# A graph layer on one core: rows of numbers for the comparisons moved to PSUM, 26 groups gathered in place of 20

## The chip, the cores and the metric

The kernel runs on one core of a Trainium2 chip. The metric is the time of one execution in microseconds of the device (us). Three runs of the kernel before took 490.9, 492.47 and 494.97 us; the median is 492.47. The core's engines are TensorE (PE in the profile, with PEld for its weight loads), VectorE (DVE), ScalarE (ACT), GpSimd (POOL) and SyncE (SP, which here only issues DMAs). Each runs its own instructions in order and waits for others by semaphores.

## The reference

One layer of a graph network over 6250 nodes with 64 features and 206250 edges, which are sorted by their destination.

```python
h = jnp.maximum(_layernorm(x, axis=-1), 0.0)
msg = h[src] + edge_feat                       # 206250 x 64
agg = jax.ops.segment_sum(msg, dst, num_segments=6250)
x = x + jax.nn.relu(agg @ W1 + b1) @ W2 + b2
```

So every node sums, over the edges that end in it, the edge's own features and the row of h of the edge's source.

## The kernel before

The edges lie in G = 202 groups of 1024. The sum over the rows of h is made in two ways. For the first GA = 182 groups it is made by **counting**: a matrix that says how often node s is the source of an edge that ends in node d is built on the chip and multiplied by h. For the last GP = 20 groups the rows of h are **gathered** by indirect DMAs that add them onto the edges' features in SBUF.

*Counting.* The nodes are taken in windows of V = 3, each with up to 128 edges in a tile. For a tile VectorE makes two one-hot matrices by comparing the edges' keys with rows of numbers 0, 1, 2, ... (`iota_lo`, 128 wide, and `iota_key`, 148 wide): `hot_lo` marks the low seven bits of the source, `hot_key` the window's node and the high bits (line 858). One pair of comparisons makes three steps of ST = 6 tiles, a batch; both hot tiles have two buffers. TensorE multiplies the two, which gives the tile's counts (`pc`, line 868), ScalarE copies the counts of a step into a ring (line 871). A step is one `count(b, s)`. A block is BT = 84 tiles, so 14 steps, and covers 252 nodes; there are NW = 23 blocks, the last with BL = 56 tiles (10 steps), 318 steps in all. In the block after, TensorE multiplies h by the counts (`multiply`, line 888, 49 products a block, into `pv`, which has two buffers in PSUM), spread over the first seven steps; VectorE adds `pv` to the sums in SBUF at step 10 (`add_products`, line 900).

*Edge features.* For the counted groups they are loaded in chunks of 42 nodes (`load`, 384 KB each, four buffers), summed by TensorE with one-hot matrices (`chunk_hot` line 427, `chunk_sum` line 439, into `bank`) and placed into `pv` (`chunk_place`, line 461).

*Gathered groups.* A group's edge rows are loaded (`load_h`, 256 KB, tile `pfeat`, four buffers, so two pairs of groups), then GpSimd issues eight gathers that add rows of h from the table in HBM (`fetch_h`, line 301 through `gather`). A pair of groups is then summed by TensorE (`features_h`, `sum_groups`, line 489), placed (`place_groups`, line 508) and added (`add_sums`). Right behind a pair's sum the loads and gathers of the pair after the next are put in the queues.

*Other gathers.* GpSimd also fetches, through the same queue and line, the words that hold the keys (`fetch_pair`, two gathers for 256 windows, `words`; `unpack_pair` and `turn_pair` make keys of them) and the nodes of the chunks' edges (`fetch_dst`, `dstq`).

*The order* is written out by hand. A loop over the steps issues `count`, then the products, placings and additions that stand at fixed steps of a block (`SUMS`, `PLACES`, `PRODUCTS`, `ADDED`; names with `_L`, and `LAST`, `LATE`, are for the last block). For GpSimd the kernel keeps a clock of its own: each gather has an assumed cost (`GATHER_US`, `WORDS_US`), each step `STEP_US`, and a pair's sum is put at the first step of a few allowed ones (`GROUPS`) at which its gathers would have landed. The clock only sets the order of instructions in the program; on the chip the engines wait for semaphores. Since TensorE runs in order, a sum that waits for its gathers holds all behind it. At the end come the rest of the products, the last sums and the two dense products of the last blocks of nodes (`mlp_hidden` line 936, `mlp_rows` line 943).

[...]

Of the kernel before, what the change touches and what calls it, by code (L numbers as in the profile page):

```python
# [9 lines left out]
F32 = mybir.dt.float32  # L10
BF16 = mybir.dt.bfloat16
# [3 lines left out]
AF = mybir.ActivationFunctionType  # L15
# [4 lines left out]
P = 128  # L20
N = 6250
E = 206250
# [12 lines left out]
J = 8  # L35
# [17 lines left out]

GP = 20
PQ = 4
PK = J // PQ
GA = G - GP
# [14 lines left out]
BT = 84  # L74
BN = V * BT
NH = BN // 2
NW = 23
BL = 56
NWIN = (NW - 1) * BT + BL - NX
NS = NWIN * V  # L80
IC = -(-NWIN // P)
# [26 lines left out]

HEAD_US = 1.5
STEP_US = 1.25  # L110
GATHER_US = 2.3
WORDS_US = 2.9
LAND_US = 4.0
NEED_P = N - 31 * GP - 6
OPEN = 30
# [6 lines left out]
def gnn_kernel(ctx: ExitStack, tc: tile.TileContext, x, src_t, dst_t, dst_g, edge, w1, b1, w2, b2, out):  # L122
# [177 lines left out]
    def gather(rows, source, index, op=OP.bypass):  # L300
        nc.gpsimd.indirect_dma_start(out=rows, out_offset=None, in_=source,  # L301
                                     in_offset=bass.IndirectOffsetOnAxis(ap=index, axis=0), compute_op=op)
# [96 lines left out]

    bank = ps.tile([P, GB * D], F32, name="bank", bufs=1)  # L400
    nc.vector.memset(bank, 0.0)
    units = []
    for b in range(NW):
        c0, c1 = (start[b] // CN, min(start[b + 1], NS) // CN)
# [240 lines left out]
    def by_quarters(t0, t1):  # L645
        rows = src_s.bitcast(F32)
        for t in range(t0, t1):
            own = slice(t * QP, (t + 1) * QP)
            px = ps.tile([P, 512], F32, tag="pv", name="psrcq")[:, :GP * PK]
            for b in range(PQ):  # L650
                nc.tensor.matmul(px, spread[own, b].rearrange("p a c -> p (a c)"), rows[own, :, b, :],
                                 start=(b == 0), stop=(b == PQ - 1))
            nc.scalar.activation(src_p[:, :, t], px.rearrange("p (g k) -> p g k", k=PK), AF.Copy)
# [28 lines left out]
    bad = small.tile([P, CHECKED + 2 * NT + 4], F32, name="bad")  # L682
    nc.vector.memset(bad, 0.0)
    sums_bad = bad[:, CHECKED + 2 * NT:]
    junk = late.tile([P, RC * CT], BF16, name="junk")

    def checked(of, p, low, high, at):
        shape = of.shape[1:]
# [156 lines left out]
    def count(b, s):  # L845

        t = b * BT + s * ST
        n = b * STEPS + s
        r = n - opens(n)
        if r == 0:  # L850
            n = min(ST * (1 if n == 0 else R - 1 if n < R else R), TILES - t)
            assert all(at_col.get(c % KR) == c for c in range(t, t + n)), t
            opened[0] = t + n
            hots[:] = [work.tile([P, R * ST, P], BF16, name="hot_lo"),
                       work.tile([P, R * ST, K + 1], BF16, name="hot_key")]
            for k, (hot, iota_k) in enumerate(zip(hots, (iota_lo, iota_key))):
                m = hot.shape[2] // 2
                nc.vector.tensor_tensor(  # L858
                    hot[:, :n].rearrange("p t (m o) -> p t m o", o=2),
                    iota_k.rearrange("p (m o) -> p m o", o=2).unsqueeze(1).to_broadcast([P, n, m, 2]),  # L860
                    keys[:, k, t % KR:t % KR + n, :].unsqueeze(2).to_broadcast([P, n, m, 2]), op=OP.is_equal)
                if k and 0 < b * STEPS + s < OPEN:
                    nc.vector.memset(spare, 0.0)
        hot_lo, hot_key = (hot[:, r * ST:(r + 1) * ST, :] for hot in hots)
        pc = ps.tile([P, 2, 512], F32, tag="pc", name="pc")
        for j in range(ST):
            k, m = divmod(j, ST // 2)
            nc.tensor.matmul(pc[:, k, m * K:(m + 1) * K], hot_lo[:, j, :], hot_key[:, j, :K],  # L868
                             start=True, stop=True)
        half, i = divmod(s, (STEPS if b < NW - 1 else STEPS_L) // 2)  # L870
        nc.scalar.activation(  # L871
            ring[:, (2 * b + half) % 3, :, i * ST * V:(i + 1) * ST * V].rearrange("p h (k m) -> p h k m", k=2),
            pc[:, :, :ST // 2 * K].rearrange("p k (m h) -> p h k m", h=HI), AF.Copy)

    def open_pv(b):
        pvs[b] = [ps.tile([P, 512], F32, tag="pv", name="pv")[:, :BN], 0]

    def multiply(b, upto):

# [99 lines left out]
    def fetch_h(g):  # L979
        if g >= G:  # L980
            return
        if g not in parts_of:
            load_h(g)
        for j in range(J):
            queue.append((GATHER_US, lambda j=j: gather(
                parts_of[g][:, j, :], table[:, :], src_p[:, g - GA, j // PK, j % PK:j % PK + 1], OP.add)))
        queue.append((0.0, lambda: fetched.setdefault(g, pool[0])))
# [102 lines left out]
    def clock(n):  # L1090

        return n * HEAD_US if n < STEPS else STEPS * HEAD_US + (n - STEPS) * STEP_US
# [6 lines left out]

    SUMS, PLACES, LAYERS = (7, 10, 13), 3, (8, 11)  # L1100
    PRODUCTS = (5, 12, 19, 26, 33, 41, HI)
    PRODUCTS_L = (8, 18, 28, 39, HI)
    ADDED, LOADED = 10, 2
    LAST, LATE, SUMS_L = (3, 8), 7, (6, 8)
    ADDS = (6, 7)
    GROUPS, PLACED = (0, 1, 2, 4), (1, 2, 4, 5)
    ready = []
# [34 lines left out]
    for n, (b, s) in enumerate(steps):  # L1142
        for f in before.get(n, []):
            f()
        count(b, s)
        upto = PRODUCTS if b < NW - 1 else PRODUCTS_L
        if b >= 1 and s < len(upto):
            multiply(b - 1, upto[s])
        if b >= 1 and s == (PLACES if b < NW - 1 else 2):
            for u in places[b - 1]:  # L1150
                chunk_place(u)
        if b >= 1 and s == (ADDED if b < NW - 1 else LATE):
            add_products(b - 1)
            if b - 1 > SB:
                ready.append(b - 1)
        k = n - (first_step[SB + 1] + ADDED + 1)
        if 0 <= k < 3 * -(-NX // 4) and k % 3 == 0:
            add_seconds(k // 3 * 4)
            if k // 3 == -(-NX // 4) - 1:
                ready[:0] = range(SB + 1)  # L1160
        if s == LOADED or b == NW - 2 and s == STEPS // 2:
            for m in ready[:len(LAYERS)] if b < NW - 1 else ready + [NW - 2, NW - 1]:
                if m not in xs:
                    residual(m)
        if b == NW - 1 and s == STEPS // 2:
            for m in range(NW, NB):
                if m not in queued:
                    residual(m)
        if s in (LAYERS if b < NW - 1 else LAST) and ready and ready[0] in xs:
            mlp(ready.pop(0), n)  # L1170
        for f in later.pop(n, []):
            f()
        if n >= 3:
            if h_next < G and s in GROUPS and fetched.get(h_next + 1, 1e9) + LAND_US <= clock(n):
                features_h(h_next)
                n_placed = next((k for k in range(n + 2, last) if b == NW - 1 or steps[k][1] in PLACED), last)
                at(n_placed, place_groups, h_next)
                h_next += GB
                add_later(next((k for k in range(n_placed + 3, last) if steps[k][1] in ADDS or steps[k][0] == NW - 1 and
                                steps[k][1] != LATE), last))  # L1180
            if n == 3:
                pool[0] = clock(n - 1) + OPENING_US
            pool_until(clock(n) + LAND_US)
# [155 lines left out]
```

## Time and profile before

| what | value |
|---|---|
| median of three runs | 492.47 us |
| the profiled execution's own time | 489.07 us |
| its span in the profile | 487.2 us |
| mean granted clock of TensorE | 0.954 |
| gathers of h (line 301, `pfeat`) | 160 |
| counts copied by ScalarE (line 871) | 318 |
| batches of comparisons (line 858) | 107 of each kind |

The profile is that of one execution. A row of a group gives the line of the code, the engine, the operation, the tile written and the tiles read, the shape and how often; behind the first bar the busy time in us and the mean in ns; behind the second the idle time of the engine just before, and what ended it. A row of the timeline gives start and duration in us, and in brackets the idle time before it. The slices cut the span into 40 equal parts of 12.2 us, one digit each, in tenths busy.

### The profile page before, as it was taken

What the parts mean: (1) busy time and instruction counts of PE and PEld (TensorE: products, weight loads), DVE (VectorE), ACT (ScalarE), POOL (GpSimd) and SP (SyncE); (2) the same over time, 40 slices, a digit from 0 to 9 for tenths busy, and PEclk for the clock granted to TensorE, in tenths of its full rate; (3) what the DMA queues carried; (4) which work ended last, traced back from release to release, by engine and by line L of the source; (5) the groups of instructions that cost most, each with busy time, mean ns of one, the idle gap of its engine ahead of it and who ended that gap; (6) DMA issues with size and microseconds to landing.
All of it is one profiled execution on the core that took longest, in us unless ns stands there. A gap on an engine that the chain in (4) does not pass through costs nothing.

```text
span 487.2 us, 17218 instructions
## 1 busy us (share of the span) xinstructions
PE 424.2 (87%) x7301; PEld 374.8 (77%) x7302; DVE 415.1 (85%) x561; ACT 366.0 (75%) x607; POOL 388.3 (80%) x239
## 2 busy tenths in 40 slices
PE   3156798998988999999999999989999999999894
PEld 3055687886886888888988978878888888888783
DVE  7888989879999798988998889888998899998751
ACT  3727889878877788788898789777887787786650
POOL 7787888888888888888888888888888888888000
PEclk9655699999999999999999999999999999999998
DMA  9959367378366585784784784675775775764700
GB/s 237 238 172 300 74 147 193 76 180 192 69 167 155 145 228 122 176 230 105 192 220 98 172 228 94 170 201 125 187 187 124 201 179 122 203 158 93 213 13 16
DMA packets 122378, 77.98 MB, mean 160 GB/s; under 512 B 34768, under 2 KB 120728, under 8 KB 122072
## 3 DMA queue, kind: packets, MB, share of 16 engines
q1 hardware_dynamic: 97464, 66.88, 47.1%
q0 software_dynamic: 24592, 9.19, 15.0%
q8 instruction: 59, 0.97, 0.8%
q10 hardware_dynamic: 240, 0.75, 0.5%
q14 instruction: 23, 0.19, 0.1%
HBM read 72.80 MB, written 3.99 MB: 158 GB/s over the span
## 4 chain that ended last, share of the span: by engine, by line
PE 68%; ACT 13%; DMA 6%; issue 5%; DVE 4%; POOL 3%; DVEq 0%; ACTq 0%; POOLq 0%
PE pv L888 26%; PE pc L868 22%; PE bank L439 11%; ACT counts L871 9%; POOL rows L301 3%; DMA feat<-in_edge 3%; PE po L943 2%; PE pv L461 2%; DMA dstq<-in_dst_g,cols_i 2%; ACT junk L694 1%; PE ph L936 1%; PE bank L489 1%; DVE hot_key L858 1%; DVE hot_lo L858 1%; DMA firsts_i<-in_dst_g 1%
## 5 line engine op out<-in xcount | busy, mean ns | idle before, releaser
L301 POOL DMA_INDIRECT pfeat<-table,src_p x160 | 334.0, 2088 | 49.7 <-issue 43.0
L871 ACT ACTIVATE counts<-pc 128x882 fp32r<-128x882 f32 x318 | 282.1, 916 | 49.1 <-PE pc L868 39.8
L868 PE MATMUL pc<-hot_key,hot_lo 128*128 128x147 bf16 x1908 | 179.2, 232 | 22.9 <-ACT counts L871 13.6
L858 DVE TENSOR_TENSOR hot_lo<-iota_lo,keys 128x2304 bf16<-128x2304 bf16 (+1 forms) x107 | 143.8, 1344 | 36.2 <-PE pc L868 29.0
L888 PE MATMUL pv<-counts,h 128*128 128x252 f32 (+1 forms) x1127 | 171.0, 292 | 0.2
L868 PEld LDWEIGHTS <-hot_lo 128*128 128x128 bf16 x1908 | 130.5, 100 | 45.4 <-issue 24.2
L858 DVE TENSOR_TENSOR hot_key<-iota_key,keys 128x2664 bf16<-128x2664 bf16 (+1 forms) x107 | 163.3, 1526 | 0.0
L888 PEld LDWEIGHTS pv<-counts,h 128*128 128x128 f32 x1127 | 143.5, 190 | 0.6 <-ACT counts L871 0.5
L439 PE MATMUL bank<-feat,hot 128*21 128x64 f32 x3240 | 69.0, 222 | 5.9 <-issue 3.0
L439 PEld LDWEIGHTS bank<-feat,hot 128*21 128x21 f32 x3240 | 52.3, 101 | 18.3 <-issue 6.8
L427 DVE TENSOR_TENSOR hot<-rel,iota 128x504 f32<-128x504 bf16 x68 | 45.6, 671 | 0.1
L442 ACT ACTIVATE by_node<-bank 128x128 f32<-128x128 f32 x68 | 19.0, 280 | 18.4 <-PE bank L439 12.4
L301 POOL DMA_INDIRECT words<-packed,first_i x15 | 20.8, 1385 | 4.6 <-issue 3.4
L301 POOL DMA_INDIRECT rows<-in_dst_g,row_i x15 | 17.4, 1162 | 5.2 <-issue 4.0
L943 PE MATMUL po<-w2s,hid 128*126 128x64 f32 (+2 forms) x100 | 16.8, 288 | 1.7 <-ACT hid L938 1.2
L943 PEld LDWEIGHTS po<-w2s,hid 128*126 128x126 f32 (+2 forms) x100 | 13.5, 192 | 5.7 <-ACT hid L938 1.9
L936 PE MATMUL ph<-sums,w1s 128*128 128x252 f32 (+2 forms) x50 | 16.1, 404 | 0.2 <-ACT y L949 0.2
L900 DVE TENSOR_TENSOR sums<-sums,pv 128x252 f32<-128x252 f32 (+4 forms) x31 | 9.8, 339 | 6.7 <-PE pv L888 5.9
L492 ACT ACTIVATE by_group<-bank 128x128 f32<-128x128 f32 x10 | 2.8, 277 | 15.1 <-PE bank L489 11.1
L938 ACT ACTIVATE hid<-ph,b1s 128x252 f32<-128x252 f32 (+2 forms) x25 | 11.6, 464 | 2.3 <-PE ph L936 2.3
L461 PE MATMUL pv<-select,by_node 128*64 128x42 f32 (+1 forms) x272 | 12.6, 234 | 0.0
L461 PEld LDWEIGHTS pv<-select,by_node 128*64 128x64 f32 x272 | 9.9, 137 | 3.0
(202 smaller groups left out, 252.3 us busy)
## 6 DMA issues: line engine op xcount, KB each, us to landing
feat<-in_edge SPq DMA_DIRECT2D x135, 384.0 KB
pfeat<-in_edge SPq DMA_DIRECT2D x20, 256.0 KB
pfeat<-table,src_p POOLq DMA_INDIRECT x160
xl<-in_x SPq DMA_DIRECT2D x2, 768.0 KB
xs<-in_x SPq DMA_DIRECT2D x23, 63.0 KB
out_y<-y SPq DMA_DIRECT2D x23, 63.0 KB
dstn<-in_dst_g SPq DMA_DIRECT2D x1, 1024.0 KB
table<-xl SPq DMA_DIRECT2D x1, 800.0 KB
```

The source lines that it names most:

```text
L301: nc.gpsimd.indirect_dma_start(out=rows, out_offset=None, in_=source, in_offset=bass.IndirectOffsetOnAxis(ap=index, axis=0), compute_op=op)
L427: nc.vector.tensor_tensor(hot_of[u][:, :n].rearrange("p c j w -> p (c j) w"), rel[:, c:c + n].rearrange("p c q k -> p (c q k)").unsqueeze( ...
L439: nc.tensor.matmul(bank[q * QP:q * QP + WQ, i * D:(i + 1) * D], hot[:, i, j, :], feat[i][:, j, :], start=(k == 0), stop=(k == JP - 1))
L442: nc.scalar.activation(by_node[u][:, :n].rearrange("p c d -> p (c d)"), bank[:, :n * D], AF.Copy)
L461: nc.tensor.matmul(pvs[b][0][i * D:(i + 1) * D, k:k + z - a], of[:, i, :], select[:, a - low:z - low], start=False, stop=False)
L858: nc.vector.tensor_tensor(hot[:, :n].rearrange("p t (m o) -> p t m o", o=2), iota_k.rearrange("p (m o) -> p m o", o=2).unsqueeze(1).to_bro ...
L868: nc.tensor.matmul(pc[:, k, m * K:(m + 1) * K], hot_lo[:, j, :], hot_key[:, j, :K], start=True, stop=True)
L871: nc.scalar.activation(ring[:, (2 * b + half) % 3, :, i * ST * V:(i + 1) * ST * V].rearrange("p h (k m) -> p h k m", k=2), pc[:, :, :ST // ...
L888: nc.tensor.matmul(pv[:, :2 * half].rearrange("p (k n) -> p k n", k=2), h2[:, h, :], of[:, :, h, :half], start=(h == 0), stop=(h == HI - 1))
L936: nc.tensor.matmul(ph[:, :n], w1s, agg[:, start[b]:start[b + 1]], start=True, stop=True)
L938: nc.scalar.activation(outs[b][:, :n], ph[:, :n], AF.Relu, bias=b1s)
L943: nc.tensor.matmul(po[:pairs[b], k, :], outs[b][:, k:2 * pairs[b]:2], w2s, start=True, stop=True)
```

## The change

Three things are changed together.

First, the numbers of `iota_lo` and `iota_key` are also written to PSUM, as 2-byte numbers: in the head TensorE turns the rows into columns by a product with ones, ScalarE copies the columns to SBUF, and TensorE transposes them into a tile `iotas` of one bank. The two comparisons of a count read their first input from there; the keys, their second input, and the outputs stay in SBUF. The bank comes from `pv`, which has one buffer from now on.

Second, GP is 26. The groups that are counted are 176 in place of 182, the blocks NW = 22, and the last has BL = 84 tiles like all others: 308 steps. The last block's own schedule becomes that of the other blocks, with `LATE` at step 11. In the last block a pair's sum may stand at any step above `LOADED`. The assumed costs of the clock go from 2.3 to 1.6 us for a gather and from 2.9 to 1.2 for a pair of words.

Third, in the last group, whose edges end within it, the gathers whose 128 rows are all padding are left out: 4 of its 8.

```diff
-GP = 20
+GP = 26
...
-NW = 23
-BL = 56
+NW = 22
+BL = 84
...
-GATHER_US = 2.3
-WORDS_US = 2.9
+GATHER_US = 1.6
+WORDS_US = 1.2
...
     bank = ps.tile([P, GB * D], F32, name="bank", bufs=1)
     nc.vector.memset(bank, 0.0)
+    iotas = ps.tile([P, P + K + 1], BF16, name="iotas", bufs=1)
+    col = ps.tile([P, 3, P], F32, tag="pc", name="pcol")
+    cols_of = late.tile([P, 3, P], BF16, name="iota_cols")
+    m = K + 1 - P
+    for k, of in enumerate((iota_lo, iota_key[:, :P], iota_key[:, P:])):
+        n = of.shape[1]
+        nc.tensor.matmul(col[:n, k, :], of[0:1, :], onesb[0:1, :], start=True, stop=True)
+        nc.scalar.activation(cols_of[:n, k, :], col[:n, k, :], AF.Copy)
+        nc.tensor.transpose(iotas[:, k * P:k * P + n], cols_of[:n, k, :], identb[:n, :n])
...
-            px = ps.tile([P, 512], F32, tag="pv", name="psrcq")[:, :GP * PK]
+            px = ps.tile([P, 512], F32, tag="pv", name="psrcq", bufs=1)[:, :GP * PK]
...
-            for k, (hot, iota_k) in enumerate(zip(hots, (iota_lo, iota_key))):
+            for k, (hot, iota_k) in enumerate(zip(hots, (iotas[:, :P], iotas[:, P:]))):
...
-        pvs[b] = [ps.tile([P, 512], F32, tag="pv", name="pv")[:, :BN], 0]
+        pvs[b] = [ps.tile([P, 512], F32, tag="pv", name="pv", bufs=1)[:, :BN], 0]
...
         for j in range(J):
+            if g * P * J + j // PK * P * PK + j % PK >= E:
+                continue
             queue.append((GATHER_US, lambda j=j: gather(
...
-    PRODUCTS_L = (8, 18, 28, 39, HI)
+    PRODUCTS_L = PRODUCTS
     ADDED, LOADED = 10, 2
-    LAST, LATE, SUMS_L = (3, 8), 7, (6, 8)
+    LAST, LATE, SUMS_L = (5, 12), 11, SUMS
...
-        if b >= 1 and s == (PLACES if b < NW - 1 else 2):
+        if b >= 1 and s == PLACES:
...
-            if h_next < G and s in GROUPS and fetched.get(h_next + 1, 1e9) + LAND_US <= clock(n):
+            if h_next < G and (s in GROUPS or b == NW - 1 and s > LOADED) and fetched.get(h_next + 1, 1e9) + LAND_US <= clock(n):
```

(One more line makes a scratch tile of ScalarE's large enough for 26 groups.)

More of the change, by code (lines that the diff above doesn't have):

```diff
@@ L684, in gnn_kernel @@
     sums_bad = bad[:, CHECKED + 2 * NT:]
-    junk = late.tile([P, RC * CT], BF16, name="junk")
+    junk = late.tile([P, max(RC * CT, 2 * GP * J)], BF16, name="junk")
     def checked(of, p, low, high, at):
```

## The prediction

> **What bounds the kernel now.** I read the page's busy times and slices first, then the chain, then the costliest groups, then the windows and the timeline around single gathers.
>
> ```profile
> span 487.2 us, 17218 instructions
> PE 424.2 (87%) x7301; PEld 374.8 (77%) x7302; DVE 415.1 (85%) x561; ACT 366.0 (75%) x607; POOL 388.3 (80%) x239
> ...
> PE   3156798998988999999999999989999999999894
> ...
> POOL 7787888888888888888888888888888888888000
> ...
> PE 68%; ACT 13%; DMA 6%; issue 5%; DVE 4%; POOL 3%; DVEq 0%; ACTq 0%; POOLq 0%
> ```
>
> From the fifth slice on TensorE is 90% busy, and the chain that ended last runs through it for two thirds: TensorE sets the end. GpSimd is 80% busy, but its last digit stands three slices before the end: it has some 36 us of room, and no more.
>
> ```profile
> 407.00:456.00 49.00, 44.95 (x851) 39.71 (x840) 43.20 (x57) 37.59 (x59) 38.96 (x19) 1.00 0.64 157
> ```
>
> These columns are PE, PEld, DVE, ACT, POOL busy, then the granted clock. In a late stretch TensorE idles 4.05 of 49 us, at full clock; what a stall costs there can hardly be won back.
>
> ```profile
> L301 POOL DMA_INDIRECT pfeat<-table,src_p x160 | 334.0, 2088 | 49.7 <-issue 43.0 <-PE pc L868 2.1 <-DMA pfeat<-table,src_p 1.8
> L858 DVE TENSOR_TENSOR hot_key<-iota_key,keys 128x2664 bf16<-128x2664 bf16 x105 | 161.6, 1539 | 0.0
> L858 DVE TENSOR_TENSOR hot_lo<-iota_lo,keys 128x2304 bf16<-128x2304 bf16 x105 | 142.3, 1355 | 36.0 <-PE pc L868 29.0 <-issue 3.6 <-ACT counts L871 1.8
> ```
>
> 160 gathers of h take 2.09 us each and 0.30 between two. The timeline shows why 2.09:
>
> ```profile
> 17.43 1.82 DVE L545 TENSOR_REDUCE stat<-xl 128x25 f32<-128x1600 f32 x1 [1.19 <-DMA xl<-in_x]
> 18.51 0.95 POOL L301 DMA_INDIRECT rows<-in_dst_g,row_i  x1 [0.30 <-ACT inrow L317]
> ...
> 20.13 1.82 DVE L550 TENSOR_TENSOR xl<-xl,stat 128x1600 f32<-128x1600 f32 x1
> 21.07 1.70 POOL L301 DMA_INDIRECT rows<-in_dst_g,row_i  x1 [0.30 <-issue]
> ...
> 107.17 1.55 POOL L301 DMA_INDIRECT pfeat<-table,src_p  x1 [0.30 <-issue]
> ...
> 213.87 1.54 DVE L858 TENSOR_TENSOR hot_key<-iota_key,keys 128x2664 bf16<-128x2664 bf16 x1
> 214.17 2.66 POOL L301 DMA_INDIRECT pfeat<-table,src_p  x1 [0.30 <-issue]
> ...
> 446.74 0.68 DVE L427 TENSOR_TENSOR hot<-rel,iota 128x504 f32<-128x504 bf16 x1
> 447.10 1.74 POOL L301 DMA_INDIRECT pfeat<-table,src_p  x1 [0.30 <-issue]
> ```
>
> A gather that begins inside a reduction, which reads one tensor, takes its usual 0.95. One that begins inside a subtraction of two SBUF tensors takes 1.70: it ends 0.82 after that operation. An adding gather with no VectorE work at all takes 1.55. Inside hot_key (ends 215.41) it ends at 216.83, 1.42 later; inside hot (ends 447.42) at 448.84, 1.42 later again. So an adding gather costs 1.54, and one that meets a VectorE operation with two SBUF inputs waits out that operation. Over 160 gathers the waiting is 334.0 - 160 x 1.54 = 87.6 us.
>
> **The change part by part.** *Rows in PSUM.* The two comparisons of a count get their first input from PSUM and keep one SBUF input, like the reduction above. I take it that they no longer hold a gather, and that they keep their 1355 and 1539 ns. No row shows 2-byte numbers read from PSUM; the nearest are 4-byte ones:
>
> ```profile
> L900 DVE TENSOR_TENSOR sums<-sums,pv 128x126 f32<-128x126 f32 x14 | 3.4, 282 | 1.9 <-PE pv L888 1.1 <-issue 0.8
> L928 DVE TENSOR_TENSOR xs<-xs,b2s 126x128 f32<-126x128 f32 x23 | 6.5, 282 | 0.0
> L427 DVE TENSOR_TENSOR hot<-rel,iota 128x504 f32<-128x504 bf16 x67 | 45.2, 675 | 0.1
> L479 DVE TENSOR_TENSOR hotp<-rel_p,iota 128x336 f32<-128x336 f32 x10 | 5.0, 501 | 0.4 <-issue 0.4
> ```
>
> 126 numbers with one input from PSUM and 128 from SBUF alone both take 282 ns: the place costs nothing there. Lower bound: no change. Upper bound: one number at a time, (675 - 501) / 168 = 1.036 ns each, against hot_lo's 1355 / 2304 = 0.59. I take the lower (the rows with PSUM are nearest); the upper is a rival.
>
> [...]
>
> Making the rows adds three products, three copies and three transposes to the head, where TensorE is 10 to 60% busy (first slices 3, 1, 5, 6) and the chain runs through GpSimd's row gathers: cost 0, at most 2 us if the copies push ScalarE's first work. For the bank that the rows take, pv has one buffer. Its next block opens at step 0, four steps after the sums were taken out at step 10; four steps are over 5 us, the two additions under 1. Cost 0; if VectorE runs late, under 1 us a block. The turning of src_p in the head shares that one buffer: four short copies in a row, under 1 us.
>
> *Ten steps less.* Blocks have 14 steps; the last had 10 and is gone.
>
> ```profile
> 406.73 0.65 PE L489 MATMUL bank<-pfeat,hotp 128*21 128x64 f32 x32
> ...
> 456.04 0.92 ACT L871 ACTIVATE counts<-pc 128x882 fp32r<-128x882 f32 x1
> ...
> 470.23 0.91 ACT L871 ACTIVATE counts<-pc 128x882 fp32r<-128x882 f32 x1
> ...
> L508 PE MATMUL placed<-sel,by_group 128*64 128x52 f32 x40 | 3.2, 240 | 0.0
> L888 PE MATMUL pv<-counts,h 128*128 128x252 f32 x1078 | 165.0, 293 | 0.1
> L888 PE MATMUL pv<-counts,h 128*128 128x180 f32 x49 | 6.0, 278 | 0.1
> ```
>
> The first count of that block is at 456.04 and its tenth at 470.23: 14.19 / 9 = 1.58 a step, 15.8 in all. Six more groups are three more pairs, each a sum of 0.65 and a placing of 3.2 / 10 = 0.32. Before the last block 8 of 10 pairs had been summed; now it is 13 of 13: five more, 5 x 0.97 = 4.9. In the tail 49 products of full width replace narrow ones: 49 x (165.0 / 1078 - 6.0 / 49) = +1.5; a pair's sum and placing leave it, -1.0. The last block's products, placings, sums and layers now stand at the steps of every other block: their cost is inside the mean step, 0 here. Edge rows only move from chunks (135 to 131 of 384 KB) to groups (20 to 26 of 256 KB), the same bytes. Against the profiled execution's 489.07, with nobody waiting: 489.07 - 15.8 + 4.9 + 0.5 = **478.7**.
>
> *The gathers.* They were 160 and are 26 x 8 - 4 = 204, the four of the padding left out (4 x 1.84 = 7.4 us at the very end of the queue). Now GpSimd's queue matters. In the order of the instructions the sums of pairs stand after 47, 85, 113, 142, 173, 211, 239, 271, 309 and 318 counts; in the changed kernel after 43, 58, 85, 100, 127, 143, 169, 187, 211, 229, 253, 271 and 295. TensorE takes its work in order: if a pair has not landed, everything behind its sum waits, products, counts, and with them ScalarE and VectorE.
>
> ```profile
> 24.32 0.95 POOL L301 DMA_INDIRECT words<-packed,first_i  x1 [0.30 <-issue]
> ...
> 45.43 1.59 POOL L301 DMA_INDIRECT pfeat<-table,src_p  x1 [1.30 <-ACT counts L871]
> 47.32 6.05 POOL L301 DMA_INDIRECT pfeat<-table,src_p  x1 [0.30 <-issue]
> ...
> 449.14 2.30 POOL L301 DMA_INDIRECT pfeat<-table,src_p  x1 [0.30 <-issue]
> ...
> 26.74 0.51 ACT L317 ACTIVATE inrow<-rows,nhalf 128x256 bf16<-128x256 int32 x1 [1.72 <-DMA rows<-in_dst_g,row_i]
> ```
>
> The twelfth pair, at count 271, decides. Its last gather is the 192nd. From 45.43: 192 x (1.54 + 0.30) = 353.3; 13 other gathers of words and nodes stand ahead of it in the queue, 13 x 1.25 = 16.3. What still has two SBUF inputs still holds some: hot is 45.2 us of the 406 in which gathers run, so 11% of them, 21, meet one and wait about half of it, 0.34: 7 us; smaller operations (xs, y, hotp, sel) 2 more. Together 9; ends are 0 and twice that. Sum 45.4 + 353.3 + 16.3 + 9 = 424.0. Landing: the row gather that ended at 22.77 let its reader start at 26.74, 4.0 later, with four times the bytes; I take 2.5, between 0 and 4. Landed at **426.5**.
>
> ```profile
> 106.77 0.64 PE L489 MATMUL bank<-pfeat,hotp 128*21 128x64 f32 x32
> ...
> 107.69 1.34 SPq L972 DMA_DIRECT2D pfeat<-in_edge  x2
> ```
>
> Each pair adds into tiles that the pair two before has freed; SyncE asks for the new rows 0.3 us after that sum. The first sum stands at count 43, some 5 us ahead of 106.77, and GpSimd is through two pairs at 45.4 + 32 x 1.84 + 1.25, near 106: cost 0, at most 3.
>
> TensorE reached count 271 at 406.73, with seven pairs behind it; with eleven it is there at 406.73 + 4 x 0.97 = 410.6. It waits 15.9. (Most of this falls at count 229, where ten pairs are due, the rest at 271.) The thirteenth pair has 12 gathers, some 23 us; TensorE needs it 24 steps later, over 30 us: no further wait. The words for the keys come behind the same gathers and get late by no more than the sums.
>
> After a wait ScalarE and VectorE have their two buffers ready, so a little comes back: 3 of the 4.05 us that TensorE idles in the late stretch. 478.7 + 15.9 - 3 = 491.6, on the scale of the profiled execution. That one lies 0.7% under the median of the runs shown (492.47; lowest 490.9), so 3.4 go on top: **495**.
>
> **The rivals.** *The gathers keep up* (faster). No hold at all, quick landing: 45.4 + 353.3 + 16.3 = 415.0 against 410.6, a wait of 4.4 that the slack takes back: 478.7 to 483, with the 3.4 up to 487; I put 483. For it: the gather at 107.17, and hot_lo and hot_key are 303.9 of VectorE's 415.1 us. Against it: the gather inside hot at 447.10, which the change leaves as it is. It needs a hold under 1 us in all.
>
> *One element at a time* (slower). Comparisons from PSUM take 675 + 1800 x 1.036 = 2540 and 675 + 2160 x 1.036 = 2913 ns in place of 1355 and 1539: 2.56 us more a batch, 104 batches, 266 us on an engine that was busy for 415 of 487. VectorE becomes the bound: 415 + 266 and its head and tail, about 700. It decides as soon as a batch of three steps takes more than three steps of TensorE, 4 us; 5.5 is beyond.
>
> *The hold stays* (the change doesn't do what it says). The gathers then run as now, (449.14 - 45.43) / 159 = 2.54 each with all else in the queue: the 192nd at 533, 125 late: about 605. Against it stands the reduction at 17.43.
>
> **How the numbers follow.** The forecast, TensorE waiting for late pairs, gets 0.60 and spans 488 to 505: 9 us less or more of hold, 1.5 of landing, a second gather like that at 47.32 (4.5). The gathers keeping up gets 0.29, one element at a time 0.06, the hold staying 0.05. The range 481 to 506 takes in the first two. A measurement of this kernel tells about 1% from no change (487.5 to 497.4): faster 0.30 (0.27 of the first rival, 0.03 of the forecast), slower 0.34 (0.23 and the two slow rivals), same 0.36.
>
> **What would show it.** Right: hot_lo and hot_key still near 1.36 and 1.54; gathers of h near 1.6 mean; 0.3 between them; waits of TensorE at the sums of pairs (pfeat) of some 10 us around 355 and more around 420; GpSimd's last gather near 447. Wrong: comparisons over 2 us; gathers still above 2; gathers under 1.5; or no wait at the sums, which would mean that I have TensorE's own pace too fast or GpSimd's start too late.

## The result

The changed kernel took 519.34 us (median of four runs, 517.75 to 520.52), the kernel before 492.89: 1.053 times as long, with an interval of 1.048 to 1.059. I had forecast 495, with a range up to 506. One thing has to be known for all that follows. Kernels were run in sessions, a few of them one after the other on one chip, always with the kernel before among them, and the times depend on the session. In four of the six sessions of experiments the kernel before took 491 to 496 us, as above, in two 470; both came up on the same chip, and what sets them is not known (the changed kernel was in all of the four and in neither of the two, so the runs can't tell whether its being there has a part in it). So each run is compared with the kernel before of its own session. Medians are of all runs; the ratios and their intervals leave out the few runs that fell in a slower state of the chip.

The page of the kernel after, busy times, slices of 12.9 us and the chain that ended last:

```profile
span 516.1 us, 17092 instructions
PE 426.2 (83%) x7200; PEld 373.1 (72%) x7201; DVE 409.0 (79%) x563; ACT 358.4 (69%) x605; POOL 368.6 (71%) x283
...
PE   1338788887987998979999598997979979999985
...
POOL 7686888858888888888888878888888887830000
...
PE 75%; ACT 11%; issue 6%; DMA 3%; DVE 3%; another core or an unknown queue 1%; ACTq 0%
```

TensorE is busy hardly longer than before (426.2 us against 424.2), in a span that is 28.9 us longer. Every engine's share fell. The chain still runs through TensorE. The groups of the kernel after, then one of the kernel before:

```profile
L301 POOL DMA_INDIRECT pfeat<-table,src_p x204 | 319.6, 1567 | 71.6 <-issue 54.5 <-PE pc L877 8.3 <-DMA pfeat<-in_edge 2.8
L867 DVE TENSOR_TENSOR hot_key<-iotas,keys 128x2664 bf16<-128x2664 bf16 x101 | 155.0, 1535 | 0.0
L867 DVE TENSOR_TENSOR hot_lo<-iotas,keys 128x2304 bf16<-128x2304 bf16 x101 | 136.9, 1355 | 63.8 <-PE pc L877 49.8 <-issue 8.5 <-PE pk L727 2.2
L451 ACT ACTIVATE by_node<-bank 128x128 f32<-128x128 f32 x66 | 18.3, 277 | 41.9 <-PE pc L877 17.0 <-PE bank L448 14.7 <-remote 5.9
```

```profile
L442 ACT ACTIVATE by_node<-bank 128x128 f32<-128x128 f32 x68 | 19.0, 280 | 18.4 <-PE bank L439 12.4 <-PE pc L868 4.0 <-PE pstart L343 1.0
```

The gathers did what was meant, 1567 ns in place of 2088, and the comparisons kept their 1355 and 1535. But ScalarE, which copies each chunk sum out of `bank` (`by_node`), now stands idle for 41.9 us ahead of these copies, not 18.4. Where that comes from shows the timeline of the kernel after around one chunk sum:

```profile
289.12 0.87 PE L448 MATMUL bank<-feat,hot 128*21 128x64 f32 x48
...
289.79 1.00 POOL L301 DMA_INDIRECT words<-packed,first_i  x1 [0.30 <-issue]
...
290.43 0.55 PE L877 MATMUL pc<-hot_key,hot_lo 128*128 128x147 bf16 x6
...
291.09 0.97 POOL L301 DMA_INDIRECT words<-packed,first_i  x1 [0.30 <-issue]
292.36 1.57 POOL L301 DMA_INDIRECT pfeat<-table,src_p  x1 [0.30 <-issue]
294.07 0.28 ACT L451 ACTIVATE by_node<-bank 128x128 f32<-128x128 f32 x1 [3.53 <-remote]
294.07 0.51 DVE L488 TENSOR_TENSOR hotp<-rel_p,iota 128x336 f32<-128x336 f32 x1 [2.04 <-remote]
```

By its records the sum ends at 289.99. Its copy, and VectorE's next operation, are let go only at 294.07, both at once, 4.1 us later; three gathers stand in between. It is the longest such delay in this trace; the next two, of 2.9 and 2.2 us, stand at pairs of gathers of words too. Added up over the 66 copies, some 28 of the 41.9 us lie behind the end of the sum's records; in the kernel before it is some 10 of 18.4. The trace alone doesn't tell whether the sum was late or only the news of its end. In the same kernel without its gathers (a run below) two such sums look so:

```profile
287.17 0.87 PE L448 MATMUL bank<-feat,hot 128*21 128x64 f32 x48
...
288.47 0.29 ACT L451 ACTIVATE by_node<-bank 128x128 f32<-128x128 f32 x1
...
290.52 0.87 PE L448 MATMUL bank<-feat,hot 128*21 128x64 f32 x48
...
291.51 0.28 ACT L451 ACTIVATE by_node<-bank 128x128 f32<-128x128 f32 x1
```

1.30 and 0.99 us from the first product to the copy. Windows of the kernel after, while gathers run and behind the last of them (columns as in the prediction, the counts in brackets):

```profile
407.00:456.00 49.00, 44.70 (x753) 39.58 (x750) 40.06 (x50) 34.30 (x60) 40.59 (x27) 1.00 0.64 147
457.00:499.00 42.00, 38.77 (x728) 34.54 (x731) 36.49 (x54) 33.49 (x52) 0.00 (x0) 1.00 0.51 147
```

With gathers TensorE got through 753 products in 49 us (15.4 a us; the kernel before 851, 17.4), without them through 728 in 42 (17.3), though its busy share is much the same, 91 and 92%. The busy time doesn't show the loss; what waits behind TensorE does.

### The profile page after: what moved, and what is told of

It reads as the page before. It is cut to its first block, busy times and chain, and to the rows that moved or that the text cites. A ratio compares the mean times of both kernels' runs of the same rounds, so it can differ in the third digit from the quotient of the medians.

```text
span 516.1 us, 17092 instructions
## 1 busy us (share of the span) xinstructions
PE 426.2 (83%) x7200; PEld 373.1 (72%) x7201; DVE 409.0 (79%) x563; ACT 358.4 (69%) x605; POOL 368.6 (71%) x283
## 3 DMA queue, kind: packets, MB, share of 16 engines
q0 software_dynamic: 30928, 10.64, 17.5%
## 4 chain that ended last, share of the span: by engine, by line
PE 75%; ACT 11%; issue 6%; DMA 3%; DVE 3%; another core or an unknown queue 1%; ACTq 0%
PE pc L877 26%; PE pv L897 24%; PE bank L448 12%; ACT counts L880 6%; PE po L952 3%; PE ph L945 2%; PE pv L470 2%; PE bank L498 2%; DMA rows<-in_dst_g,row_i 1%; PE psrcq L660 1%; DMA firsts_i<-in_dst_g 1%; DMA feat<-in_edge 1%; DVE hot_lo L867 1%; ACT srcl L604 1%
## 5 line engine op out<-in xcount | busy, mean ns | idle before, releaser
L301 POOL DMA_INDIRECT pfeat<-table,src_p x204 | 319.6, 1567 | 71.6 <-issue 54.5
L880 ACT ACTIVATE counts<-pc 128x882 fp32r<-128x882 f32 x308 | 272.2, 916 | 48.8 <-PE pc L877 38.5
L867 DVE TENSOR_TENSOR hot_lo<-iotas,keys 128x2304 bf16<-128x2304 bf16 (+1 forms) x104 | 139.3, 1340 | 64.7 <-PE pc L877 50.6
L897 PE MATMUL pv<-counts,h 128*128 128x252 f32 x1078 | 165.6, 294 | 0.7 <-issue 0.6
L867 DVE TENSOR_TENSOR hot_key<-iotas,keys 128x2664 bf16<-128x2664 bf16 (+1 forms) x104 | 157.7, 1517 | 0.0
L897 PEld LDWEIGHTS pv<-counts,h 128*128 128x128 f32 x1078 | 138.9, 191 | 1.2 <-issue 0.7
L451 ACT ACTIVATE by_node<-bank 128x128 f32<-128x128 f32 x66 | 18.3, 277 | 41.9 <-PE pc L877 17.0
L301 POOL DMA_INDIRECT words<-packed,first_i x15 | 15.3, 1019 | 4.6 <-issue 4.3
L952 PE MATMUL po<-w2s,hid 128*126 128x64 f32 (+2 forms) x100 | 17.3, 296 | 0.7 <-ACT hid L947 0.6
L909 DVE TENSOR_TENSOR sums<-sums,pv 128x252 f32<-128x252 f32 (+2 forms) x29 | 9.5, 346 | 7.2 <-PE pv L897 7.2
L945 PEld LDWEIGHTS ph<-sums,w1s 128*128 128x128 f32 x50 | 7.7, 195 | 8.8 <-ACT y L958 5.2
L470 PE MATMUL pv<-select,by_node 128*64 128x42 f32 x262 | 12.1, 235 | 0.0
```

The source lines that it names most:

```text
L451: nc.scalar.activation(by_node[u][:, :n].rearrange("p c d -> p (c d)"), bank[:, :n * D], AF.Copy)
L470: nc.tensor.matmul(pvs[b][0][i * D:(i + 1) * D, k:k + z - a], of[:, i, :], select[:, a - low:z - low], start=False, stop=False)
L867: nc.vector.tensor_tensor(hot[:, :n].rearrange("p t (m o) -> p t m o", o=2), iota_k.rearrange("p (m o) -> p m o", o=2).unsqueeze(1).to_bro ...
L880: nc.scalar.activation(ring[:, (2 * b + half) % 3, :, i * ST * V:(i + 1) * ST * V].rearrange("p h (k m) -> p h k m", k=2), pc[:, :, :ST // ...
L897: nc.tensor.matmul(pv[:, :2 * half].rearrange("p (k n) -> p k n", k=2), h2[:, h, :], of[:, :, h, :half], start=(h == 0), stop=(h == HI - 1))
L945: nc.tensor.matmul(ph[:, :n], w1s, agg[:, start[b]:start[b + 1]], start=True, stop=True)
```

## The experiments

Theory A at first: gathers hold up TensorE's 4-byte sums, more so when VectorE doesn't hold the gathers. Theory B: VectorE's reading from PSUM slows TensorE. Theory C: pv's one buffer and the longer head. Theories D, E and F came up on the way and are told in the expectations.

**The parts of the change.** The kernel before with the new rows in PSUM, and, as a second kernel, without the last of these edits, so with the bank given up and the rows written but read from SBUF:

```diff
+    iotas = ps.tile([P, P + K + 1], BF16, name="iotas", bufs=1)
...
-        pvs[b] = [ps.tile([P, 512], F32, tag="pv", name="pv")[:, :BN], 0]
+        pvs[b] = [ps.tile([P, 512], F32, tag="pv", name="pv", bufs=1)[:, :BN], 0]
...
-            for k, (hot, iota_k) in enumerate(zip(hots, (iota_lo, iota_key))):
+            for k, (hot, iota_k) in enumerate(zip(hots, (iotas[:, :P], iotas[:, P:])))
```

> The kernel before with the rows of numbers in PSUM (and pv in one buffer, which they need); 20 groups, 23 blocks and the order of the steps stay. Theory A (gathers block TensorE's 4-byte sums: the trace after has the completions of chunk sums and pair sums only in the last 0.35 us of a gather and up to 0.3 us behind it; gathers that nothing holds leave TensorE shorter free stretches): slower than before, a block of 14 steps 19.5 to 21 us while gathers run in place of 18.7, 500 to 515 us in all. Theory B (VectorE's reading from PSUM slows TensorE's writing to PSUM): slower as well, 510 to 525 us, and evenly, also where no gathers run. Theory C (one buffer of pv and the longer head): the same as the kernel with one buffer alone. My prediction's own view (nothing of this costs TensorE anything): 490 to 495 us.

> The kernel before with pv and psrcq in one buffer and the rows of numbers written to PSUM in the head, but the comparisons still read them from SBUF. Theories A and B: only the head is longer, by 2 to 6 us: 492 to 499 us, a block 18.7 us as before. Theory C: most of the loss is here, 505 to 520 us, with waits at the first step of each block.

Measured beside a kernel before of 469.9: 475.56 (ratio 1.010, 1.007 to 1.013) and 475.01 (1.009, 1.007 to 1.012). Beside that kernel before, reading the rows from PSUM costs 0.5 us, and the bank and the head cost 5.1, nothing like 27. But a session of 470 may have had no such loss to explain, so this alone doesn't decide theories B and C for a session of 492. A run further down says more: without gathers of h the changed kernel, with its rows in PSUM and pv in one buffer, takes 472.62 in such a session, so neither costs 27 us by itself.

**Without gathers of h.**

```diff
-            queue.append((GATHER_US, lambda j=j: gather(
-                parts_of[g][:, j, :], table[:, :], src_p[:, g - GA, j // PK, j % PK:j % PK + 1], OP.add)))
+            queue.append((GATHER_US, lambda j=j: None))
```

> The changed kernel without the 204 gathers of h (the rows of h of the last 26 groups are left out of the sums; their edge rows are loaded and summed as ever). Theory A: a block takes 17.2 to 18.2 us from the third block to the end, as it does after 457 us in the changed kernel, 450 to 472 us in all. Theory B: a block keeps 20.5 to 21.5 us, 505 to 520 us in all.

> The kernel before without its 160 gathers of h (left out of the sums in the same way). Theory A: gathers cost the kernel before something too, but less, since VectorE holds them: a block 17.5 to 18.2 us in place of 18.7, 465 to 482 us in all. Theory B: no change in the blocks, 486 to 493 us.

466.88 and 470.20, in the same session as above. The kernel before is no faster without its gathers there, against theory A. So the sessions came into question:

> The changed kernel once more, beside the kernel before, since on the chip of the last four runs the kernel before takes 470 us and not 492, and leaving out its gathers changes nothing there. Theory A1 (gathers hold up TensorE's 4-byte sums on the chip of the first comparison, not on the chip of the last four): where the kernel before takes about 470 us, the changed kernel takes 465 to 474, a ratio of 0.99 to 1.01; where it takes about 492, 515 to 522. Theory A2 (only gathers that nothing holds, 1.87 us apart, hold up the sums, on every chip): 490 to 500 us against 470, a ratio of 1.045 to 1.06 on each chip.

518.35 beside 491.68 (1.058, 1.049 to 1.068), as theory A1 forecast. But the chip was the one on which the kernel before had taken 469.9, so it isn't the chip. Theory A2, a cost everywhere, fails by the 475.56. Then the disputed cost by itself: streams of products, alone and beside gathers.

```diff
+                for u in range(20):
+                    for i in range(2):
+                        for k in range(3):
+                            for q in range(4):
+                                nc.tensor.matmul(px[q * 32:q * 32 + 21, i * D:(i + 1) * D], hot[:, q * 3 + k, :],
+                                                 feat[:, q * 3 + k, :], start=(k == 0), stop=(k == 2))
```

> A kernel of its own that measures the disputed cost (it computes nothing of the reference): TensorE runs five kinds of streams, each once alone, once beside adding gathers and once beside plain gathers of 128 rows of 256 bytes. The kinds: 20 chunk sums as in the kernel, 4-byte (960 products of 21 columns by 64); the same with 2-byte operands; 80 products of 128 by 512, 2-byte; 24 of them, 4-byte; 440 of 128 by 64, 2-byte. Where the kernel before takes about 492 us: theory A, that gathers hold up 4-byte operands: the two 4-byte streams are slower beside gathers, by 1.5 times or more, the others not. Theory D, that gathers hold up TensorE where it gets many short instructions: the two kinds of sums and the 128 by 64 stream are slower, the two of 512 columns not. Theory B: no stream is slower beside gathers. Where the kernel before takes about 470 us, all theories expect no difference over 5%.

> The changed kernel without its gathers of h once more, since its first run stood beside a kernel before of 470 us. Theory A (and D): 462 to 472 us wherever it runs, so nearly 50 us under the 518 of the changed kernel where the kernel before takes 492. Theory B, or anything that lies in the program itself: about 51 us over its first run there, 510 to 520.

> The kernel before without its gathers of h once more. Theories A and D: 468 to 475 us, also where the kernel before takes 492: the whole difference between its 470 and its 492 is what its gathers cost TensorE. Otherwise: 488 to 495 there.

> The kernel before with the rows of numbers in PSUM once more (20 groups). Where the kernel before takes 492 us: theories A and D expect 500 to 512, since its gathers are no longer held and come closer together while they run, though they end earlier; if the time is lost by the six more groups or by the last block's order, 495 to 499 (the longer head alone, 5 us).

Again a kernel before of 469.85. Streams: no difference but the second's (9.5 alone, 10.5 beside adding gathers; 26.8 and 26.2, 17.5, 20.9 and 13.0 the others, twice each). The 10% of the second is over the 5% expected, but another stream, alone, differs by 1.1 us from session to session (26.8 here, 25.7 below). The rest as before: 465.75, 470.21 and 475.49 (1.013, 1.009 to 1.018). So the next were run beside the changed kernel:

> The changed kernel a third time. So far it stood beside a kernel before of 492 us twice; the runs without gathers stood beside one of 470. Theory E (in some sessions, whatever the program, gathers hold up TensorE; in others not): if the kernel before takes 492 here, 515 to 522; if it takes 470, 468 to 476, the six groups' 11 us and the longer head's 5 cancelling most of each other. Theory F (the changed program itself slows TensorE, wherever it runs): 500 or more beside 470.

> The streams alone and beside gathers once more. In the session where the kernel before took 470 us the five streams took 26.8, 9.5, 17.5, 20.9 and 13.0 us alone and 26.2, 10.5, 17.5, 20.9 and 13.0 beside adding gathers. If the kernel before takes 492 here: theory A (4-byte operands): the first and fourth take half as long again beside gathers or more; theory D (many short instructions): the first, second and fifth do; theory B: none does. If it takes 470: as before within 5%.

> The changed kernel without its gathers of h. Where the kernel before takes 470 it took 466. If the kernel before takes 492 here: theories A, D and E: still 463 to 472 us, so that all of the loss hangs on the gathers; theory F: 500 or more.

519.59 beside 490.92 (1.059, 1.052 to 1.066). The changed kernel without gathers: 472.62, 47.0 less. That is 0.6 above the range of theories A, D and E, and 6 to 7 above its own 466.88 and 465.75; the gathers that are left in it (of words, rows and nodes) may be why, which wasn't run. Its row of the copies behind the chunk sums:

```profile
L451 ACT ACTIVATE by_node<-bank 128x128 f32<-128x128 f32 x66 | 18.7, 284 | 4.6 <-PE bank L448 4.6
```

Theory F (the program itself) falls: without its gathers of h the changed kernel loses nothing to the kernel before. Where the kernel before takes 491, the streams differ. TensorE's timeline of the second stream beside adding gathers, in the session of 470 and then, a part of it, in that of 491:

```profile
205.16 2.83 PE L80 MATMUL px<-feat_dt.bfloat,hot_dt.bfloat 128*21 128x64 bf16 x246 [1.32 <-DVE feat_dt.bfloat L65]
209.81 1.81 PE L80 MATMUL px<-feat_dt.bfloat,hot_dt.bfloat 128*21 128x64 bf16 x128 [1.82 <-issue]
213.81 1.73 PE L80 MATMUL px<-feat_dt.bfloat,hot_dt.bfloat 128*21 128x64 bf16 x106 [2.19 <-issue]
```

```profile
229.71 0.86 PE L80 MATMUL px<-feat_dt.bfloat,hot_dt.bfloat 128*21 128x64 bf16 x49 [0.47 <-issue]
230.82 0.29 PE L80 MATMUL px<-feat_dt.bfloat,hot_dt.bfloat 128*21 128x64 bf16 x6 [0.25 <-issue]
231.58 0.85 PE L80 MATMUL px<-feat_dt.bfloat,hot_dt.bfloat 128*21 128x64 bf16 x48 [0.47 <-issue]
232.67 0.28 PE L80 MATMUL px<-feat_dt.bfloat,hot_dt.bfloat 128*21 128x64 bf16 x6 [0.25 <-issue]
```

TensorE now works in time with the gathers, which start every 1.85 us: some 54 products for each, then a stop of 0.47 us. Beside plain gathers, of 0.95 us with the same gap of 0.30, hardly one goes through a gather: in the 24.1 us from 305.70 to 329.84, with a gather every 1.25 us, the records have 15. The same stream there, and the last gathers:

```profile
329.63 0.21 PE L80 MATMUL px<-feat_dt.bfloat,hot_dt.bfloat 128*21 128x64 bf16 x1 [2.59 <-issue]
...
335.23 0.21 PE L80 MATMUL px<-feat_dt.bfloat,hot_dt.bfloat 128*21 128x64 bf16 x1 [1.89 <-issue]
335.93 0.23 PE L80 MATMUL px<-feat_dt.bfloat,hot_dt.bfloat 128*21 128x64 bf16 x2 [0.49 <-issue]
336.63 3.32 PE L80 MATMUL px<-feat_dt.bfloat,hot_dt.bfloat 128*21 128x64 bf16 x233 [0.47 <-issue]
```

```profile
328.79 0.94 POOL L70 DMA_INDIRECT into<-in_x,at_sum_copy  x1 [0.30 <-issue]
330.04 0.94 POOL L70 DMA_INDIRECT into<-in_x,at_sum_copy  x1 [0.30 <-issue]
```

The jam dissolves 5.6 us after the last gather's end (330.98). From a stream's first product to ScalarE's copy behind its last, in us:

| stream | alone | adding gathers | plain gathers |
|---|---|---|---|
| sums, 4-byte | 25.7 | 31.0 | 69.4 |
| sums, 2-byte | 9.3 | 14.6 | 54.6 |
| 128 x 512, 2-byte | 17.5 | 17.5 | 47.4 |
| 128 x 512, 4-byte | 20.9 | 20.9 | 28.3 |
| 128 x 64, 2-byte | 13.0 | 14.8 | 59.0 |

Beside adding gathers the three streams of many short products are slower, whatever their type, by 1.21, 1.57 and 1.14 times; the two of 512 columns are not. So A falls, which named the first and the fourth, and B, which named none. Of D, which asked half as long again of all three, the direction holds and the size only for the second. Beside plain gathers all are slower, the long products too, which D didn't have. Of the third, TensorE's row and ScalarE's copy:

```profile
449.17 17.44 PE L84 MATMUL px<-big_dt.bfloat 128*128 128x512 bf16 x78 [1.72 <-DVE big_dt.bfloat L67]
```

```profile
496.53 0.22 ACT L95 ACTIVATE copied<-px 128x64 f32<-128x64 f32 x1 [92.12 <-remote]
```

By its records it is through at 466.6; ScalarE's copy begins 30 us later, the picture seen above at the chunk sum. The last gather of that stage ended at 490.90, so the copy comes 5.6 us behind it, as the end of the jam did above. Whether the products themselves were late, or only the news of their end, these runs don't tell apart. In the kernel the chunk sums and pair sums are such streams, 48 and 32 products in under a microsecond, and the gathers of words, which stood at that long stop, are plain.

**Number or manner.** Still open was why the changed kernel pays more for its gathers.

> The changed kernel beside the three that follow. It has so far stood beside a kernel before of 491 to 493 us each time (518 to 520 itself), and the sessions without it beside one of 470. Theory E (the session decides, the program does not): either 518 beside 492 or, where the kernel before takes 470, 468 to 476. Theory F: over 500 even beside 470.

> The kernel before with the rows of numbers in PSUM, 20 groups. Beside a kernel before of 492: if every gather costs TensorE the same (22 us for the 160 of the kernel before, 0.14 each), 495 to 499, the longer head alone; if gathers that are not held and follow each other after 0.3 us cost it more each, 502 to 512. Beside 470: 475 as twice before.

> The kernel before without its gathers of h. Beside a kernel before of 492: theories A, D and E expect 470 to 476, so that gathers cost the kernel before some 18 to 22 us too; if its 492 came from anything else in such a session, 486 or more.

Beside a kernel before of 490.64: the changed kernel 508.69 (one run, 10 under what was expected), the kernel before without gathers 477.59, with the rows in PSUM and 20 groups 512.06 (1.044, 1.038 to 1.049). So the gathers cost the kernel before 13.0 us too, less than the 18 to 22 expected (one run), and 160 gathers that VectorE doesn't hold cost 512.06 - 477.59 - 5.1 (bank and head) = 29.4. That is 0.18 us for each gather in place of 0.08. So the manner counts. At 0.18 the 204 gathers of the changed kernel would cost 37.5; beside the 490.64 they cost about 36 (508.69 - 472.62, the latter from the session of after_third), beside the 490.92 they cost 47.0. How much the greater number adds differs by session. The row of the copies behind the chunk sums, without gathers and with the rows in PSUM:

```profile
L442 ACT ACTIVATE by_node<-bank 128x128 f32<-128x128 f32 x68 | 19.4, 285 | 5.3 <-remote 3.7 <-PE bank L439 1.6
```

```profile
L451 ACT ACTIVATE by_node<-bank 128x128 f32<-128x128 f32 x68 | 19.0, 279 | 35.0 <-PE pc L877 15.1 <-PE bank L448 15.0 <-PE po L952 3.3
L301 POOL DMA_INDIRECT pfeat<-table,src_p x160 | 252.0, 1575 | 140.5 <-PE pc L877 57.4 <-issue 42.9 <-DMA pfeat<-in_edge 18.0
```

ScalarE's idle time ahead of these copies is thus 5.3 us without gathers, 18.4 in the kernel before, 35.0 with the rows in PSUM and 41.9 in the changed kernel. In the session of 470 the very same program with the rows in PSUM had 2.4:

```profile
L451 ACT ACTIVATE by_node<-bank 128x128 f32<-128x128 f32 x68 | 19.4, 285 | 2.4 <-PE bank L448 2.0
```

Who ended a wait is known less surely in the one than in the other: of that program the trace holds 5968 semaphore updates (the records from which the profile infers who ended a wait) in the session of 492, 8668 and 8635 in the two of 470.

Is it that gathers which nothing holds follow each other too closely? A filling behind each was to spread them:

```diff
+    spacer = small.tile([1, 560], F32, name="spacer")
...
+            queue.append((GATHER_US, lambda j=j: (gather(
...
+                nc.gpsimd.memset(spacer, 0.0))))
```

> The same, with a filling of 560 zeros in one partition by GpSimd behind each gather of h, about 0.6 us, so that a gather and its gap take about 2.4 us as in the kernel before. Beside a kernel before of 492: if each gather costs the same, the same time as the kernel without the filling, within 3 us; if the shortness of the free stretch between two gathers costs the time, 494 to 499, at least 5 us under it. Beside 470: 474 to 478, as without the filling.

512.49 beside 490.64 (1.045, 1.038 to 1.052), but the gathers weren't spread. GpSimd's timeline:

```profile
200.26 1.56 POOL L301 DMA_INDIRECT pfeat<-table,src_p  x1 [0.27 <-issue]
201.25 0.61 POOL L997 MEMSET spacer<- 1x560 f32 x1
202.13 1.58 POOL L301 DMA_INDIRECT pfeat<-table,src_p  x1 [0.27 <-issue]
```

The filling runs beside the gather's last 0.6 us, and the next starts 1.87 us after it as ever. So once more with 1000 zeros, and the changed kernel for the session:

> The kernel before with the rows of numbers in PSUM, 20 groups, and a filling of 1000 zeros behind each gather of h. The filling of 560 did not spread the gathers: it ran beside the last 0.6 us of the gather, and starts stayed 1.86 us apart. This one begins about 1.0 us after a gather's start and takes about 1.03, so that starts come some 2.3 us apart, like the median of the kernel before (2.32). Beside a kernel before of 492: if the short free stretch between gathers that nothing holds is what costs the time (512 without spreading), 494 to 502; if it is something else about gathers that are not held, or the rows in PSUM, 508 to 516.

> The changed kernel beside the run that follows, for the session: every session with it so far had the kernel before at 491 to 493, and both sessions without it at 470. If that holds, 508 to 520 here beside 490 to 493.

```profile
199.90 1.57 POOL L301 DMA_INDIRECT pfeat<-table,src_p  x1 [0.30 <-issue]
200.89 0.92 POOL L997 MEMSET spacer<- 1x1000 f32 x1
201.97 1.56 POOL L301 DMA_INDIRECT pfeat<-table,src_p  x1 [0.16 <-issue]
```

2.07 us now, not the 2.3 meant, and 512.09 beside 496.25 (1.037, 1.018 to 1.055); the changed kernel took 520.22. No gain that can be told, and nothing like the 494 to 502 of the theory. That closeness costs the time isn't borne out, though 0.2 us more is a weak test of it; larger gaps weren't tried. What it is about a held gather that costs TensorE less stays open. With the rows in PSUM two things change at once: VectorE no longer holds the gathers (1575 ns in place of 2088), and VectorE reads PSUM beside them. These runs don't part the two.

## Why the prediction was wrong

*Ten steps less, five more pair sums* (-15.8, +4.9, +0.5, so -10.4): about right. Without gathers the changed kernel took 3.3, 4.5 and 5.0 us less than the kernel before, each from one run of either, the third pair from two sessions; with the 5.1 of bank and head put back that is 8.4, 9.6 and 10.1.

*Making the rows, one bank* (0, at most 2 if the copies push ScalarE's first work, and under 1 for the turning of src_p): too small. They cost 5.1 (one_bank), most of it by the first of these terms. ScalarE's first work on the sources in the kernel before, then in the kernel after, with the gather of rows that waits behind it:

```profile
5.17 1.42 ACT L589 ACTIVATE src<-src 128x1456 f32<-128x1456 int32 x1 [1.47 <-DMA src<-in_src_t]
```

```profile
9.37 0.28 ACT L409 ACTIVATE iota_cols<-pcol 128x128 bf16<-128x128 f32 x1 [4.88 <-PE pcol L408]
...
11.28 1.36 ACT L598 ACTIVATE src<-src 128x1408 f32<-128x1408 int32 x1
...
21.87 0.95 POOL L301 DMA_INDIRECT rows<-in_dst_g,row_i  x1 [3.11 <-ACT inrow L317]
```

The copies that make the rows wait for their products, one by one, and push this work back by 6.1 us. The gather of rows that stands at 21.87 began at 18.51 before, and the turning of src_p begins 4.5 us later than before. What is left of 6.1, some 1.6, falls to the turning itself:

```profile
38.26 1.89 PE psrcq L660 x8
...
40.17 0.23 ACT src_p L662
...
40.44 1.96 PE psrcq L660 x8
```

These are its second and third set of products. In its one buffer a set waits for the copy of the set before, and each takes nearly 2 us. The first count comes at 45.34 in place of 39.25. pv's one buffer cost nothing: from the third block to the twentieth one_bank takes 17.95 us a block, by the starts of the first counts, the kernel before without gathers 17.92 in the same session.

*The gathers.* Rows in PSUM no longer hold them: right. A gather that begins at 287.93, inside hot_key (286.80 to 288.34), takes 1.55 us. The mean is 1567 ns; 319.6 - 204 x 1.54 = 5.4 us of holding are left where I had 9. Comparisons at 1355 and 1535: right, and the second rival is out. The twelfth pair, forecast to land at 426.5:

```profile
50.10 1.59 POOL L301 DMA_INDIRECT pfeat<-table,src_p  x1 [2.72 <-ACT src_p L662]
...
431.63 1.55 POOL L301 DMA_INDIRECT pfeat<-table,src_p  x1 [0.30 <-issue]
...
452.23 0.64 PE L498 MATMUL bank<-pfeat,hotp 128*21 128x64 f32 x32
```

Its last gather ended at 433.18, 9 late to my 424.0, of which 4.7 are the later start. But the sum that I saw waiting for it from 410.6 stood only at 452.23. **TensorE was late, not the gathers**; the wait of 15.9, and the 3 that I let come back, were not there.

*"With nobody waiting: 478.7"* is the step that failed. It took TensorE's pace from a trace in which gathers ran and left it unchanged when they came without being held and in greater number, as if a gather could cost TensorE only by being late. In the sessions of 492 its gathers cost the changed kernel 519.59 - 472.62 = 47.0 us and the kernel before 490.64 - 477.59 = 13.0, 34.0 more. With -10.4 and +5.1 that makes 28.7, and 28.7 was measured (519.59 - 490.92). This agreement is worth little: it says hardly more than that 472.62 lies 5.0 below 477.59, where -10.4 and +5.1 make 5.3. The 13.0 and the 5.1 are from other sessions, and in the session of the 13.0 the changed kernel was only 18.1 behind (508.69 - 490.64). I had named the sign, no wait at the sums, but given it no rival and no chance. The profile before held a hint: `by_node` idled 18.4 us, about half of it for sums whose records had ended. And in a session of 470 all of this is absent; for the changed kernel that was only seen without gathers.

The second stream, 9.3 us alone and 14.6 and 54.6 beside gathers, was held up in one kind of session and hardly in the other (9.5 and 10.5, 9.8). Where it is held up the runs don't show.

## What to carry to other kernels

An engine's pace that was read from a trace held here only for what ran beside it (TensorE got through 17.4 products a us beside the gathers of the kernel before, 15.4 beside those of the changed one): before a transfer is made denser, look for work that ends later than its records say (here a copy that waits on a finished sum), and run the kernel once without the transfers to see what they cost the others. Bursts of short products were the first to be held up here (9.3 us became 14.6); a stream of long ones beside the same adding gathers lost nothing (17.5 us with and without them). And a comparison needs its own kernel before from the same session: here 470 and 492 stood for the same program.

## What was not expected of the hardware

- In some sessions indirect gathers hold up TensorE: 480 short products took 9.3 us alone, 14.6 beside adding gathers, 54.6 beside plain ones, and the copy behind 80 long products began 30 us after the end of their records. In another session, on another chip, next to nothing of it (9.5, 10.5 and 9.8). The chip alone doesn't decide it: one chip had the kernel before at 469.9 and at 491.68. What does isn't known.
- A filling by GpSimd begins about 1.0 us after the start of an adding gather of 1.56 and runs beside the rest of it.
- VectorE's comparisons of 128x2304 and 128x2664 numbers, with their 2-byte rows read from PSUM against keys in SBUF, took 1355 and 1535 ns, with both from SBUF 1355 and 1539.
